# A decoder layer on one core: score tiles, bank split, weight pool and transpose path changed together

## The chip, the core and the metric

The kernel runs on one of the eight cores of a Trainium2 chip. The metric is device time in microseconds (us) for one execution. Times given for a kernel without further words are medians of several runs; views of the profile come from one profiled execution. The names of the engines are those of the profile: PE is TensorE's matmul side (PEld its weight loads), DVE is VectorE, ACT is ScalarE, POOL is GpSimd, SP is SyncE, which here does nothing but issue DMAs.

## The reference

Everything is fp32. Three blocks follow each other, each with its own layer norm and residual, on `x` of shape (4, 1024, 256):

```python
x = x + self_attention(layernorm(x))      # 16 query heads, 4 key/value heads of 64, softmax over 1024 keys, not causal
x = x + cross_attention(layernorm(x), ctx)  # 16 heads of 16, 64 context rows
x = x + routed_ffn(layernorm(x))          # the router picks one of 64 small splines for each row

# self-attention
xq = xq * scale;  xk, xv = repeat(xk, 4), repeat(xv, 4)
scores = einsum('bqhd,bkhd->bhqk', xq, xk)
probs  = softmax(scores)
out    = einsum('bhqk,bkhd->bqhd', probs, xv).reshape(B, S, 1024) @ o_w.T + o_b
```

The 4 x 16 x 1024 x 1024 scores of the self-attention are nearly all of the work.

## The kernel before

**Tiles and steps.** For each of the 4 batch rows there are 8 query tiles of 128 rows. Heads are taken in pairs: the two heads of a pair lie on partitions 0-63 and 64-127 (`halves`) and use a key/value head each. A *step* is one pair of heads with one query tile; two steps make a *duo* (function `duo`, L566): four heads, 4 x 1024 weights per query row. There are 256 steps and 128 duos.

**One step.** Four matmuls (L592) fill two score tiles `s` of 128x1024, one for each head and two PSUM banks each. For each tile DVE finds the negated row maximum (`nmax`, L606) and ACT takes the exponential (L612), which writes the weights into the duo's tile `prob` (128x4096) and adds the row sums into `sums`. The next step's scores need both tiles free, since there are two in all.

**Turning the weights.** The value product AV (L671) contracts over keys, so it needs the weights with the keys on partitions. There are two ways. Where `by_array(d)` holds (every fourth duo, L458), PE turns 128x128 blocks with an identity (`ptp`, L631, a "flip") into PSUM and ACT copies them (L635) into `probT`. In the other duos DVE transposes the 32x32 blocks in place (L621, one instruction for a head), and sixteen DMAs, the carries (L648), move the blocks between groups of 32 partitions from `prob` to `probT`:

```python
643            for k in range(4):
644                for qb in range(4):
645                    r = (qb + k) % 4
...
648                        nc.sync.dma_start(
649                            out=probT.t[32 * r : 32 * r + 32, S * qb : S * (qb + 1)],
650                            in_=prob.t[32 * qb : 32 * qb + 32, S * r : S * (r + 1)],
651                        )
```

Every carry waits for all four transposes of its duo, and AV for all sixteen carries. There are two `prob` and two `probT` tiles.

**After AV.** AV runs in two parts of eight matmuls into a PSUM tile `av` (L659), ACT copies it to `heads` (L686). When the four duos of a query tile are there, `project` (L691) divides by the row sums, which travel through DRAM to be spread over partitions (`rsT`, `rsD`, `rb`), and multiplies by the output weights (`po`, L728).

**Everything else** is spread between these steps: layer norms with their transposes (`ln_pt`, L441), projections of queries (`pq`, L545), keys and values (`pk`, `pv`), cross-attention for two query tiles at a time (`pxq`, `xs`, `pxt`, `xav`, `pxp`, L797), and the feed-forward for four query tiles at a time (`pch`, `pcomp`, `pr` and a long series of small DVE operations, L1023; nine calls).

**PSUM.** Eight banks: `ps_s` has two tiles of two banks for the scores, `ps_1` three single banks (tag `p1`, function `psum1`) for all of the rest but AV, and `ps_o` one for AV. `xs` takes two of the single banks at once.

**The order.** Nothing is scheduled by hand or by the compiler: each operation is handed to a planner with `add(engine, cost, key, emit, reads, writes, ...)`. `Flow.order` (L120) simulates the six queues with the given costs, a lag from one engine to the next (`LAG`, L87), a count of places for each kind of tile (`places`, L228), and always emits the operation that could start first; among equals an `urgent` one, then the lower key. Tiles of one kind are taken in order of the keys of their first users, unless the kind is in `shared`. An operation that isn't urgent is put off if an urgent one would come up while it runs (L153):

```python
153                        if not t.urgent and start < soon < start + t.cost - self.SLACK:
154                            start = soon
```

What the planner emits is the program order of each engine; at run time the semaphores decide, and each queue keeps that order. Places are counted in the plan only: the pools hand out their buffers in turn.

Of the kernel before, what the change touches and what calls it, by code (L numbers as in the profile page):

```python
# [56 lines left out]
class Buf:  # L57


    def __init__(self, tag=None, make=None, whole=None):  # L60
        self.tag, self.make, self.whole = tag, make, whole or self
        self.writers, self.readers, self.parts = [], [], {}
        self.uses, self.first, self.left, self.last, self.t = set(), None, 0, 0.0, None

# [13 lines left out]
class Flow:  # L78
# [7 lines left out]
    AHEAD, SLACK = 16, 0.4  # L86
    LAG = {"PE": 0.3, "DVE": 0.2, "ACT": 0.25, "POOL": 0.25}  # L87
# [32 lines left out]
    def order(self):  # L120
        free = {tag: [0.0] * n for tag, n in self.places.items()}
# [14 lines left out]
        while todo:  # L136
            best = None
            for engine, some in could.items():
                pick = None
                soon = min((t.ready for t in some if t.urgent), default=inf)  # L140
                for t in some:
                    if t.key > front + self.AHEAD:
                        continue
                    start = max(now[engine], t.ready)
                    seen = {}
                    for b in t.takes:
                        k = seen[b.tag] = seen.get(b.tag, -1) + 1
                        line = self.lines.get(b.tag)
                        if len(free[b.tag]) <= k or (line and line[k] is not b):
                            break  # L150
                        start = max(start, free[b.tag][k])
                    else:
                        if not t.urgent and start < soon < start + t.cost - self.SLACK:  # L153
                            start = soon
                        rank = (start, not t.urgent, t.key, t.number)
                        if pick is None or rank < pick[0]:
                            pick = (rank, t)
                if pick and (best is None or pick[0] < best[0]):
                    best = pick
# [5 lines left out]
            for b in t.takes:  # L165
                free[b.tag].pop(0)
# [10 lines left out]
            for b in t.bufs:  # L177
                b.left -= 1
                b.last = max(b.last, t.end)
                if not b.left:  # L180
                    insort(free[b.tag], b.last + 0.2)
            yield t

    def emit(self):
        for t in self.order():
            for b in t.takes:
                b.t = b.make()
# [5 lines left out]
def decoder(  # L193
# [26 lines left out]
    ps_s = ctx.enter_context(tc.tile_pool(name="ps_s", bufs=2, space=PSUM))  # L220
    ps_1 = ctx.enter_context(tc.tile_pool(name="ps_1", bufs=3, space=PSUM))
    ps_o = ctx.enter_context(tc.tile_pool(name="ps_o", bufs=1, space=PSUM))
# [5 lines left out]
            s=2, p1=3, o=1, x=3, xn1=2, xT=1, kT0=1, kT1=1, vn=4, qT=12, prob=2, probT=2, sums=3, nmax=4,  # L228
# [8 lines left out]
    def buf(tag, pool, *shape, bufs=None, name=None):  # L237
        bufs = flow.places[tag] if bufs is None else bufs
        return Buf(tag, lambda: pool.tile([P, *shape], F32, tag=tag, name=name or tag, bufs=bufs))

    def psum1(name):

        return Buf("p1", lambda: ps_1.tile([P, 512], F32, tag="p1", name=name))
# [159 lines left out]
    def layernorm(key, name, src, dst, w, reads, writes):  # L403

        st = Buf("ln", lambda: (
            small.tile([P, w, 6], F32, tag="bnst", name=f"{name}_st", bufs=2),
            small.tile([P, w, 2], F32, tag="bnmv", name=f"{name}_mv", bufs=2),
            small.tile([P, w], F32, tag="bnrs", name=f"{name}_rs", bufs=2),
# [20 lines left out]
        add("DVE", 0.6 * w, key, stats, reads, [st], holds=writes)  # L429
        add("POOL", 1.0, key, rsqrt, [st], [st])  # L430
        add("ACT", 0.45 * w, key, apply, [st, *reads], writes)

    def transposed(key, name, src, dst, k, reads, write):
# [12 lines left out]
        add("PE", 0.55, key, flips, reads, [pt], holds=[write])  # L446
# [9 lines left out]
    def by_array(d):  # L456

        return d % 4 == 3  # L458
# [27 lines left out]
    def keys(b, j, key):  # L486

        kT = kTs[b, j] = buf(f"kT{j}", big, S, name=f"kT_{b}_{j}")
        for g in range(2):
# [15 lines left out]
            add("PE", 1.75, key, project, [wk_, xTs[b].part(2 * g), xTs[b].part(2 * g + 1)], [pk], holds=[kT])  # L505
            add("ACT", 0.7, key, evict, [pk, colv_], [kT])

    def value_rows(b, g, key):
# [24 lines left out]
        add("PE", 1.75, key, project, [wv_, xTs[b].part(g)], [pv], holds=[vn])  # L533
        add("DVE", 0.69, key, evict, [pv, rowv_], [vn])

    def queries(b, w, c, key):
# [16 lines left out]
        add("PE", 1.8, key, project, [wq_, xTs[b].part(w)], [pq], holds=[qTs[b, w, c], qTs[b, w, c + 1]])  # L553
# [12 lines left out]
    def duo(b, d):  # L566
# [7 lines left out]
        prob = Buf("prob", lambda: work.tile([P, 4 * S], F32, tag="prob", name=f"prob_{b}_{d}"))  # L574
        probT = Buf("probT", lambda: work.tile([P, 4 * S], F32, tag="probT", name=f"probT_{b}_{d}"))
# [7 lines left out]
        for i in range(2):  # L583
# [3 lines left out]
            ps = [Buf("s", lambda z=z: ps_s.tile([P, S], F32, tag="s", name=f"s_{b}_{d}_{i}_{z}")) for z in range(2)]  # L587
# [12 lines left out]
            add("PE", 1.95, n - 3, scores, [q, kT], ps, holds=[prob, ss], lead=True)  # L600
            for z in range(2):
# [14 lines left out]
                add("DVE", 1.22, n - 3, largest, [ps[z]], [nmax], urgent=True)  # L616
                add("ACT", 1.33, n - 3, exponential, [ps[z], nmax], [prob.part((z, i)), ss.part(k)], urgent=True)
                if not by_array(d):
# [4 lines left out]
                    add("DVE", 1.25, n - 1, turn, [prob.part((z, i))], [prob.part((z, i))])  # L623
                else:
                    for g in range(2):
# [11 lines left out]
                        add("PE", 0.54, n - 1, flips, [prob.part((z, i))], [pt], holds=[probT])  # L637
                        add("ACT", 0.6, n - 1, evict, [pt], [probT.part((z, g))])

        if not by_array(d):  # L640


            for k in range(4):
                for qb in range(4):
                    r = (qb + k) % 4

                    def carry(qb=qb, r=r):
                        nc.sync.dma_start(  # L648
# [5 lines left out]
                        "SP", 0.6, at, carry, [prob.part((z, i)) for z in range(2) for i in range(2)],  # L654
# [4 lines left out]
        av = Buf("o", lambda: ps_o.tile([P, 2 * P], F32, tag="o", name=f"av_{b}_{d}"))  # L659
        jp = e // 2  # L660
        for part in range(2):
            def values(part=part):
                for kc in range(4 * part, 4 * part + 4):
                    for z, r in enumerate(halves):
# [3 lines left out]
                        else:  # L668
# [3 lines left out]
                            av.t[r, :],  # L672
# [7 lines left out]
                "PE", 1.9, at + 1, values,  # L680
# [4 lines left out]
        def evict():  # L685
            nc.scalar.copy(hd.t.rearrange("p c q -> p (c q)"), av.t)  # L686

        add("ACT", 0.45, at + 1, evict, [av], [hd])


    def project(b, qt):  # L691
# [4 lines left out]
        rT = Buf("rsT", lambda: small.tile([H, P], F32, tag="rsT", name=f"rsT_{b}_{qt}", bufs=1))  # L696
        rD = Buf("rsD", lambda: dram.tile([2, QC, P], F32, tag="rsD", name=f"rsD_{b}_{qt}"))
# [21 lines left out]
        for z, r in enumerate(halves):  # L719
            add("SP", 0.5, at - 4, lambda z=z, r=r: spread(z, r), [rD], [rb.part(z)], lag=2.5)  # L720
        for e in range(QC // 2):
            add("POOL", 0.6, at - 1, lambda e=e: divide(e), [rb.part(0), rb.part(1), hT[e]], [hT[e]])
        xb = x_part(b, qt)
        po, t = psum1(f"po_{b}_{qt}"), buf("res", work, D, name=f"res_{b}_{qt}")
        for part in range(2):
# [4 lines left out]
            add("PE", 1.75, at, out_rows, hT[2 * part : 2 * part + 2] + [wo_] + [po] * part, [po], holds=[t])  # L730
# [66 lines left out]
    def cross_attention(b, t0, at):  # L797
# [27 lines left out]
        add("PE", 1.8, at + 1, project_q, [xT, xwq_], [pq], holds=[qT])  # L825
# [3 lines left out]
        for k in range(TX):  # L829
# [15 lines left out]
            add("PE", 1.1, now, scores, [qT, kblk], ps, holds=[sc])  # L845
            for z in range(2):
# [9 lines left out]
                add("DVE", 0.75, now, masked, [ps[z], mneg_], [sc])  # L856
# [30 lines left out]
            add("POOL", 1.6, now + 1, add_up, [sc], [half], holds=[rs])  # L887
# [34 lines left out]
            add("PE", 0.9, now + 3, values, [pT.part(0), pT.part(1), vblk], [av], holds=[oT])  # L922
# [18 lines left out]
            add("PE", 0.9, now + 4, project_o, [oT, xwo_], [po], holds=[r])  # L941
# [4 lines left out]
    def calibrated(at, name, score, w, reads):  # L946
# [3 lines left out]
        def new(tag, *shape):  # L950
            return small.tile([P, *shape], F32, tag=tag, name=f"{name}_{tag}", bufs=1)

        c = Buf("cal", lambda: (
            new("cf", n), new("chot", NK - 1, n), new("clow", n), new("cpick", NK - 1, n), new("cval0", n), new("cval1", n),
# [45 lines left out]
    def first_max(at, name, g, n, reads):  # L1000

        m = Buf("fm", lambda: (
            small.tile([P, n], F32, tag="fm", name=f"{name}_m", bufs=4),
            small.tile([P, n, NCL], F32, tag="fw", name=f"{name}_w", bufs=4),
# [18 lines left out]
    def feed_forward(b, t0, w, at):  # L1023
# [3 lines left out]
        xf = Buf("xf", lambda: big.tile([P, w, D], F32, tag="xf", name=f"ln3_{name}_n"))  # L1027
        xT = Buf("fxT", lambda: big.tile([P, DC, n], F32, tag="fxT", name=f"ln3_{name}_T"))
# [13 lines left out]
        hT = Buf("hT", lambda: big.tile([COMP, n], F32, tag="hT", name=f"hT_{name}"))  # L1042
        ph, pc = psum1(f"pch_{name}"), psum1(f"pcomp_{name}")
        comp = Buf("comp", lambda: small.tile([P, w, 2], F32, tag="comp", name=f"comp_{name}", bufs=2))
# [26 lines left out]
        sc = Buf("sc", lambda: small.tile([P, w, NS], F32, tag="sc", name=f"sc_{name}", bufs=1))  # L1071
        pr = psum1(f"pr_{name}")

        def route():
# [18 lines left out]
        hot = Buf("hot", lambda: (  # L1093
            small.tile(wide, F32, tag="hot", name=f"hot_{name}", bufs=1),
            small.tile([P, w, TPC], F32, tag="sel", name=f"sel_{name}", bufs=2),
            small.tile([P, w], F32, tag="tno", name=f"tno_{name}", bufs=1),
            small.tile([P, w], mybir.dt.int32, tag="tile", name=f"tile_{name}", bufs=1),
# [22 lines left out]
        par = Buf("par", lambda: big.tile([P, w, GT], F32, tag="par", name=f"par_{name}"))  # L1120
        for t in range(w):
# [8 lines left out]
            add("POOL", 1.2, at + 11, gather, [hot], [par.part(t)], lag=3.0)  # L1130


        hh = Buf("hh", lambda: (
            small.tile([P, w, GRID], F32, tag="hh", name=f"hh_{name}", bufs=1),
            small.tile([P, w, GRID], F32, tag="h2", name=f"h2_{name}", bufs=1),
            small.tile([P, w], F32, tag="mag", name=f"mag_{name}", bufs=1),
# [166 lines left out]
```

## Time and profile before

| | us |
|---|---|
| median of 3 runs | 1982.43 (1979.98 to 1986.18) |
| the profiled execution, own time | 1978.13 |
| its span, first to last instruction | 1976.4 |
| PE busy | 1737.7 |
| DVE busy | 1400.9 |
| ACT busy | 1062.5 |
| POOL busy | 554.1 |
| first scores start at | 36.8 |
| last scores start at | 1867.4 |
| mean granted TensorE clock | 0.939 |

Busy times are unions over an engine's instructions; issuing DMAs isn't in them. The row of a group has the busy time of all its instructions, the mean duration of one in ns, and the engine's idle time just before them with the instruction that ended it. fp32 matmuls appear as two records each, so a step's four score matmuls are eight records.

### The profile page before, as it was taken

How to read it: one execution, taken by the hardware profiler on the slowest of the kernel's cores; microseconds unless marked ns; L12 is line 12 of the kernel's file. 1: busy time of each engine (PE TensorE's matmuls, PEld its weight loads, DVE VectorE, ACT ScalarE, POOL GpSimd, SP SyncE). 2: the span in 40 equal slices, each digit the busy share in tenths (PEclk: the TensorE clock that was granted, in tenths of full speed). 3: DMA queues.
4: the chain of work that ended last, by engine and by line, in shares of the span. 5: the costliest groups of instructions: out<-in, count | busy, mean ns of one | idle time of the engine just before them, and what ended most of it. 6: DMA issues, size and time to landing. Idle time of an engine off the chain costs nothing.

```text
span 1976.4 us, 28894 instructions
## 1 busy us (share of the span) xinstructions
PE 1737.7 (88%) x10180; PEld 1025.7 (52%) x10180; DVE 1400.9 (71%) x2036; ACT 1062.5 (54%) x1977; POOL 554.1 (28%) x872
## 2 busy tenths in 40 slices
PE   6898989889998998989999898988999899997842
PEld 4455555555654555555655454555555455554521
DVE  4667777886778766787677676787677876778632
ACT  3445556656564655655565555655565455555511
POOL 1001213152122512225031522316122350304352
PEclk8889999999998999999999898999999899999965
DMA  3566455455655455566454456545555645445500
GB/s 131 128 139 150 115 140 122 115 146 125 138 129 136 106 137 124 121 152 150 102 134 107 123 136 139 139 116 126 136 116 116 157 118 129 105 111 130 139 23 12
DMA packets 95455, 243.05 MB, mean 123 GB/s; under 512 B 28368, under 2 KB 39376, under 8 KB 95312
## 3 DMA queue, kind: packets, MB, share of 16 engines
q1 hardware_dynamic: 91504, 229.39, 49.6%
q0 software_dynamic: 2704, 9.46, 1.7%
q10 hardware_dynamic: 1104, 2.37, 0.3%
q8 instruction: 81, 1.33, 0.3%
q14 instruction: 62, 0.51, 0.1%
HBM read 35.32 MB, written 4.46 MB: 20 GB/s over the span
## 4 chain that ended last, share of the span: by engine, by line
PE 64%; DVE 16%; ACT 6%; POOL 5%; DMA 3%; SPq 3%; issue 3%; POOLq 0%; DVEq 0%; ACTq 0%
PE s L592 22%; PE av L671 18%; DVE nmax L606 6%; PE pq L545 5%; PE po L728 4%; PE ptp L631 4%; DVE prob L621 3%; SPq L648 3%; ACT prob L612 3%; PE pk L494 1%; PE pv L517 1%; DMA par<-in_table,tile 1%; PE pxt L898 1%; PE xs L837 1%; PE pxq L814 1%
## 5 line engine op out<-in xcount | busy, mean ns | idle before, releaser
L606 DVE TENSOR_REDUCE nmax<-s 128x1 f32<-128x1024 f32 x512 | 601.9, 1216 | 342.7 <-PE s L592 341.4
L612 ACT ACTIVATE prob<-s,nmax 128x1024 f32<-128x1024 f32 x512 | 568.8, 1114 | 407.3 <-DVE nmax L606 388.7
L592 PE MATMUL s<-kT,qT 64*128 64x512 f32 x2048 | 584.4, 639 | 35.0 <-ACT prob L612 34.6
L671 PE MATMUL av<-probT,vn 128*64 128x256 f32 x4096 | 499.4, 396 | 29.5 <-DMA probT<-prob 26.0
L621 DVE STREAM_TRANSPOSE prob<-prob 128x1024 f32<-128x1024 f32 x384 | 458.6, 1223 | 37.7 <-ACT prob L612 26.8
L671 PEld LDWEIGHTS av<-probT,vn 128*64 128x64 f32 x4096 | 298.2, 142 | 252.3 <-issue 111.7
L592 PEld LDWEIGHTS s<-kT,qT 64*128 64x128 f32 x2048 | 212.9, 192 | 266.5 <-issue 163.6
L710 POOL TENSOR_TENSOR heads<-heads,rb 128x256 f32<-128x256 f32 x128 | 90.0, 729 | 607.6 <-DMA rb<-rsD 503.7
L635 ACT COPY probT<-ptp 128x512 f32<-128x512 f32 x256 | 137.8, 590 | 74.3 <-PE ptp L631 72.5
L631 PE MATMUL ptp<-ident,prob 128*128 128x128 f32 x1024 | 141.1, 281 | 34.0 <-ACT prob L612 30.4
L631 PEld LDWEIGHTS ptp<-ident,prob 128*128 128x128 f32 x1024 | 112.8, 143 | 82.4 <-issue 37.6
L545 PE MATMUL pq<-ln_T,wq 128*128 128x256 f32 x512 | 127.6, 394 | 12.3 <-DVE xsc L849 12.3
L863 POOL TENSOR_TENSOR xsc<-xsc,xmx 128x1024 f32<-128x1024 f32 x32 | 61.2, 1914 | 248.2 <-DVE xmx L860 136.7
L728 PE MATMUL po<-wo,heads 128*128 128x256 f32 x512 | 119.2, 383 | 1.6 <-POOL heads L710 1.6
L545 PEld LDWEIGHTS pq<-ln_T,wq 128*128 128x128 f32 x512 | 95.3, 194 | 47.9 <-issue 29.2
L728 PEld LDWEIGHTS po<-wo,heads 128*128 128x128 f32 x512 | 95.5, 190 | 29.8 <-POOL heads L710 9.2
L612 ACT ACTIVATION_READ_ACCUMULATOR prob<-s,nmax 128x1 f32 x512 | 101.0, 197 | 0.0
L427 ACT ACTIVATE ln_n<-x,ln_mv,ln_rs 128x256 f32<-128x256 f32 x64 | 36.6, 596 | 107.1 <-POOL ln_mv L422 107.1
L686 ACT COPY heads<-av 128x256 f32<-128x256 f32 x128 | 47.6, 372 | 76.3 <-PE av L671 73.9
L556 ACT ACTIVATE qT<-pq,bqs,qscale 128x256 f32<-128x256 f32 x128 | 65.6, 564 | 35.6 <-PE pq L545 35.5
L419 POOL TENSOR_SCALAR ln_rs<-ln_mv 128x1 f32<-128x1 f32 (+1 forms) x96 | 21.4, 222 | 213.2 <-DVE ln_mv L415 200.7
L441 PE MATMUL ln_pt<-ident,ln_n 128*128 128x128 f32 x192 | 37.2, 312 | 44.9 <-ACT ln_n L427 42.4
(166 smaller groups left out, 1498.1 us busy)
## 6 DMA issues: line engine op xcount, KB each, us to landing
probT<-prob SPq DMA_DIRECT2D x1536, 128.0 KB, 2.3
rb<-rsD SPq DMA_DIRECT2D x64, 256.0 KB, 3.9
ln_n<-in_x SPq DMA_DIRECT2D x16, 256.0 KB, 3.1
x<-in_x SPq DMA_DIRECT2D x8, 512.0 KB, 4.9
out<-ln_n POOLq DMA_DIRECT2D x7, 512.0 KB, 4.9
wq<-in_w_qT ACTq DMA_DIRECT2D x1, 1024.0 KB, 8.0
wo<-in_w_oT SPq DMA_DIRECT2D x1, 1024.0 KB, 12.6
rowv<-in_rows ACTq DMA_DIRECT2D x1, 774.0 KB, 10.6
```

What stands on the lines that cost most here:

```text
L545: mm(pq.t[:, 2 * P * k : 2 * P * (k + 1)], lhsT=wq[:, dc, (c + k) * P : (c + k + 1) * P], rhs=xTs[b].t[:, dc, 2 * P * w : 2 * P * (w + 1)] ...
L556: nc.scalar.activation(qTs[b, w, c + k].t, pq.t[:, 2 * P * k : 2 * P * (k + 1)], AF.Identity, bias=bqs[:, c + k : c + k + 1], scale=qscale,)
L592: mm(ps[z].t[:, 512 * g : 512 * (g + 1)], lhsT=q.t[r, (qt % 2) * P : (qt % 2 + 1) * P], rhs=kT.t[r, 512 * g : 512 * (g + 1)], start=True, ...
L606: nc.vector.tensor_reduce(nmax.t, ps[z].t, AX.X, ALU.max, negate=True)
L612: nc.scalar.activation(weights(prob.t, z, i), src, AF.Exp, bias=nmax.t, accum_out=ss.t[:, k : k + 1])
L621: nc.vector.transpose(t, t)
L631: flip(pt.t[:, j * P : (j + 1) * P], weights(prob.t, z, i)[:, kc * P : (kc + 1) * P], ident)
L635: nc.scalar.copy(to[:, z, 4 * g : 4 * g + 4, i, :], pt.t.rearrange("p (c q) -> p c q", q=P))
L671: mm(av.t[r, :], lhsT=vns[b, kc // 2].t[:, kc % 2, j * HD : (j + 1) * HD], rhs=rhs, start=(kc == 0), stop=(kc == NT - 1),)
L710: nc.gpsimd.tensor_tensor(hT[e].t, hT[e].t, rb.t[:, 2 * e : 2 * e + 2, :], ALU.mult)
L728: mm(po.t[:, :D], lhsT=hT[c // 2].t[:, c % 2], rhs=wo[:, c, :], start=(c == 0), stop=(c == QC - 1))
L863: nc.gpsimd.tensor_tensor(sc.t, sc.t, mx.t.unsqueeze(2).to_broadcast([P, XH, SK]), ALU.subtract)
```

## The change

- **Score tiles.** `ps_s` has three tiles of two banks, still one for each head. `ps_1` has two single banks instead of three, and AV takes one of them (`psum1`) instead of its own.
- **Weight tiles.** `prob` and `probT` come from one pool of four tiles.
- **Transposes.** `by_array` is always false: every duo is turned by DVE and carried by DMA; PE's flips and their copies are gone.
- **Two queues.** Of a duo's sixteen carries the last four (`k == 3`) are issued on ACT's queue, the other twelve on SP's as before.
- **Buffers by place.** The planner notes which place a tile was given, and the tile is made from that place's own buffer (`f"{tag}_{k}"`, one buffer each), so plan and program use the same one.
- **Planner.** The rule at L153 is dropped; lags between engines are about halved; a place is free 0.1 us after its last use instead of 0.2; some twenty costs are changed by a few hundredths to half a us.

The core of the diff; the new tags of all other tiles follow the same pattern:

```diff
-    AHEAD, SLACK = 16, 0.4
-    LAG = {"PE": 0.3, "DVE": 0.2, "ACT": 0.25, "POOL": 0.25}
+    AHEAD = 16
+    LAG = {"PE": 0.15, "DVE": 0.1, "ACT": 0.1, "POOL": 0.15}
...
-        free = {tag: [0.0] * n for tag, n in self.places.items()}
+        free = {tag: [(0.0, k) for k in range(n)] for tag, n in self.places.items()}
...
-                soon = min((t.ready for t in some if t.urgent), default=inf)
...
-                        if not t.urgent and start < soon < start + t.cost - self.SLACK:
-                            start = soon
...
-                free[b.tag].pop(0)
+                b.place = free[b.tag].pop(0)[1]
...
-                    insort(free[b.tag], b.last + 0.2)
+                    insort(free[b.tag], (b.last + 0.1, b.place))
...
-                b.t = b.make()
+                b.t = b.make(b.place)
...
-    ps_s = ctx.enter_context(tc.tile_pool(name="ps_s", bufs=2, space=PSUM))
+    ps_s = ctx.enter_context(tc.tile_pool(name="ps_s", bufs=1, space=PSUM))
     ps_1 = ctx.enter_context(tc.tile_pool(name="ps_1", bufs=3, space=PSUM))
-    ps_o = ctx.enter_context(tc.tile_pool(name="ps_o", bufs=1, space=PSUM))
...
-            s=2, p1=3, o=1, x=3, xn1=2, xT=1, kT0=1, kT1=1, vn=4, qT=12, prob=2, probT=2, sums=3, nmax=4,
+            s=3, p1=2, x=3, xn1=2, xT=1, kT0=1, kT1=1, vn=4, qT=12, prob=4, sums=3, nmax=4,
...
     def by_array(d):
 
-        return d % 4 == 3
+        return False
...
-        prob = Buf("prob", lambda: work.tile([P, 4 * S], F32, tag="prob", name=f"prob_{b}_{d}"))
-        probT = Buf("probT", lambda: work.tile([P, 4 * S], F32, tag="probT", name=f"probT_{b}_{d}"))
+        prob = Buf("prob", lambda k: work.tile([P, 4 * S], F32, tag=f"prob_{k}", name=f"prob_{b}_{d}", bufs=1))
+        probT = Buf("prob", lambda k: work.tile([P, 4 * S], F32, tag=f"prob_{k}", name=f"probT_{b}_{d}", bufs=1))
...
-            add("PE", 1.95, n - 3, scores, [q, kT], ps, holds=[prob, ss], lead=True)
+            add("PE", 1.93, n - 3, scores, [q, kT], ps, holds=[prob, ss], lead=True)
...
-                add("DVE", 1.22, n - 3, largest, [ps[z]], [nmax], urgent=True)
-                add("ACT", 1.33, n - 3, exponential, [ps[z], nmax], [prob.part((z, i)), ss.part(k)], urgent=True)
+                add("DVE", 1.17, n - 3, largest, [ps[z]], [nmax], urgent=True)
+                add("ACT", 1.14, n - 3, exponential, [ps[z], nmax], [prob.part((z, i)), ss.part(k)], urgent=True)
...
-                    add("DVE", 1.25, n - 1, turn, [prob.part((z, i))], [prob.part((z, i))])
+                    add("DVE", 1.19, n - 1, turn, [prob.part((z, i))], [prob.part((z, i))])
...
-                    def carry(qb=qb, r=r):
-                        nc.sync.dma_start(
+                    engine, queue, cost = ("ACT", nc.scalar, 0.45) if k == 3 else ("SP", nc.sync, 0.68)
+
+                    def carry(qb=qb, r=r, queue=queue):
+                        queue.dma_start(
...
-                        "SP", 0.6, at, carry, [prob.part((z, i)) for z in range(2) for i in range(2)],
+                        engine, cost, at, carry, [prob.part((z, i)) for z in range(2) for i in range(2)],
...
-        av = Buf("o", lambda: ps_o.tile([P, 2 * P], F32, tag="o", name=f"av_{b}_{d}"))
+        av = psum1(f"av_{b}_{d}")
```

## The prediction

> **What bounds the kernel now.** I read the page's busy line first, then the busy time in three stretches, then the groups of instructions with the waits in front of them, then SP's own waits and the DMA in one burst. The page:
>
> ```profile
> PE 1737.7 (88%) x10180; PEld 1025.7 (52%) x10180; DVE 1400.9 (71%) x2036; ACT 1062.5 (54%) x1977; POOL 554.1 (28%) x872
> PE 64%; DVE 16%; ACT 6%; POOL 5%; DMA 3%; SPq 3%; issue 3%; POOLq 0%; DVEq 0%; ACTq 0%
> ```
>
> TensorE is the busiest engine and holds 64% of the chain that ended last; VectorE comes next. The busy times by stretch (engines in the order PE, PEld, DVE, ACT, POOL, then clock, DMA share, GB/s) cut the span at the first scores (37 us) and the last scores (1867 us):
>
> ```profile
> 37.00:1867.00 1830.00, 1675.28 (x9901) 985.42 (x9903) 1351.64 (x1844) 1026.39 (x1910) 506.98 (x767) 0.96 0.55 128
> 0.00:37.00 37.00, 21.26 (x58) 12.46 (x60) 10.92 (x54) 13.13 (x25) 7.88 (x44) 0.86 0.52 175
> 1867.00:1976.00 109.00, 41.13 (x227) 27.80 (x223) 38.36 (x138) 22.99 (x43) 39.28 (x61) 0.63 0.06 17
> ```
>
> The middle decides: PE 1675 of 1830 us (91.5%), 155 us idle; DVE 1352 us (74%). Its 256 steps (one per pair of heads and query tile) take 7.15 us each. The head and the tail are latency and hardly change. The groups (busy, mean ns | idle just before, and who ended it):
>
> ```profile
> L606 DVE TENSOR_REDUCE nmax<-s 128x1 f32<-128x1024 f32 x512 | 601.9, 1216 | 342.7 <-PE s L592 341.4
> L592 PE MATMUL s<-kT,qT 64*128 64x512 f32 x2048 | 584.4, 639 | 35.0 <-ACT prob L612 34.6
> L671 PE MATMUL av<-probT,vn 128*64 128x256 f32 x4096 | 499.4, 396 | 29.5 <-DMA probT<-prob 26.0
> L621 DVE STREAM_TRANSPOSE prob<-prob 128x1024 f32<-128x1024 f32 x384 | 458.6, 1223 | 37.7 <-ACT prob L612 26.8
> L635 ACT COPY probT<-ptp 128x512 f32<-128x512 f32 x256 | 137.8, 590 | 74.3 <-PE ptp L631 72.5
> L631 PE MATMUL ptp<-ident,prob 128*128 128x128 f32 x1024 | 141.1, 281 | 34.0 <-ACT prob L612 30.4
> ```
>
> DVE's 342.7 us of waiting are for scores, so PE paces it. PE's own waits are small and each has an owner: 35.0 us of scores waiting for an exponential to free a score tile, 34.0 in front of the flips of every fourth duo, 29.5 in front of AV. Last, the carries:
>
> ```profile
> SPq L648 <- DVE prob L621: 386.2, 84, 11.1
> probT<-prob SPq DMA_DIRECT2D x1536, 128.0 KB, 2.3
> 1073.00:1082.00 9.00, 5.95 (x26) 3.92 (x24) 8.61 (x18) 3.39 (x6) 0.72 (x1) 1.00 0.88 198
> ```
>
> SP waits 386 us for transposes, so it has room. Inside one burst of 16 carries (10.06 us in the timeline) the 16 DMA engines are already 0.88 busy at 198 GB/s.
>
> **What the Trainium skill says.** "DMA: Bandwidth & Descriptors", section "Issuing engines are not separate DMA queues": DMAs of SP and ACT run on the same 16 engines, and a second issuer saves only issue time. The 0.88 of that burst agrees: the second queue can shorten it by about an eighth at most, 10.1 to 9 us. "TensorE: Matmul & The Clock Gate", "What's actually happening": the clock halves after about 3.4 us of idle time. Agrees: after 3.25 us idle at 618.71 us, eight score matmuls took 4.91 us, against 1.99 without a gap. The same page, "Architectural detail", calls ACT and DVE strict FIFO, so a carry on ACT holds up what stands behind it; no run here shows a carry on ACT. "PSUM — Partial Sum Buffer", "PSUM: the matmul accumulator", counts 8 banks: 4+3+1 become 6+2, with none left over; the trace cannot show banks.
>
> **The change, part by part.**
> *Flips out.* 32 duos lose 1024 flips: −141.1 us of PE, all on the bounding engine, and −34.0 us of waits in front of them. On ACT their 256 evictions (137.8 us) go too.
> *Block transposes in.* 32 × 4 = 128 more, × 1.223 = +156.5 us of DVE. Middle: PE 1675−137 (the flips that lie in it) = 1538, DVE 1352+156 = 1508. They are now equal, and DVE's slack of 26% falls to 10%. It is no direct cost, since it lies in the 342.7 us that DVE waited. The cover is thin, though: a maximum (L606) more often meets a transpose and waits half of 1.22 us. Extra chance (0.90−0.74) × 0.61 × 512 = 50 us; I let half reach PE: +25 (bounds 0 and 100).
> *Carries.* 16 × 32 = 512 more DMAs. SP keeps its number (12 × 128 = 1536, median issue 0.59 us, so 7.1 us a duo of 12.9). ACT gets 4 × 128 = 512, at the 0.45 us of its weight loads at the start: +230 us of queue. ACT: 1062−138+230 = 1154 us, under the other two, so nothing while DVE is on time; behind an ACT carry that waits for a late transpose stand exponentials, and PE waits for those. That is in the +25. DMA share 0.55 × 4/3 over a shorter time is about 0.8: a longer landing than 2.3 us, which goes into AV's 29.5 us of waits. I leave these unchanged: later landings against one pool of four tiles. That pool lets the next duo take a tile before the last carry has been read; no row shows this wait apart (bounds −26 and +30).
> *Third score tile.* One head of the next step can start after the first exponential. Of 35.0 us of waits I take 70%: −25 (bounds −35 and 0).
> *Two banks for all the rest.* Takes after: AV 128, pq 64, xs 64, pxt 64, ln_pt 48, po, pxp, xav, rsT 32 each, others 83: 579, which share two banks instead of three plus AV's own. PE fills them 1738−141−584 = 1013 us. Adding an eviction and about half a us of waiting to each fill gives some 1760 us of occupancy, so 1.3 us of turnover a take, and two banks are 53% full over 1670 us (before: about 29% of three). Before, only pq and pxp waited for a bank behind xs (12.8 us). I take +25, 0.04 us a take; bounds 0 and 240 (rival C).
> *Clock.* The mean score matmul was 639 ns against a median of 589; fewer long gaps: −10 (bounds −40, +20).
> *Last duo.* It was a flipped one. Now: two last transposes 2.4, twelve issues 7.1, landing 2.3 put its AV about 6 us later: +6.
> *Order.* The planner's costs, shorter lags and the dropped reservation for urgent work move queues around; no row prices this: 0, within ±30.
>
> Sum against the profiled span: 1976.4−141.1−34.0−25−10+25+25+6 = 1822. Its own time was 1978.1, 1.7 above the span; the median of the runs shown is 1982.4, 4.3 above that. So **1828 us**. The middle becomes about 1670 us: PE 92%, DVE 90%, 6.5 us a step.
>
> **The rivals.**
> A, *the cushions work*: three score tiles and four weight tiles cover DVE and banks, and PE reaches 94%: 1538/0.94 = 1636, +37 +115 = 1788, 1794 as a median. For: PE's idle time before is mostly short waits with owners that go. Against: DVE at 92%.
> B, *DVE becomes the bound in bursts*: the router and spline work of the feed-forward (9 calls) kept DVE full between 600 and 628 us already; there PE stood 3.25 us. If each call holds the scores 8 us longer than planned: +72, 1900.
> C, *two banks starve PE* (slower): the 272 short fills (ln_pt, xs, pxt, xav, pxp, rsT, some 0.65 us each) don't cover a turnover of 1.3, and each loses 0.65 us: 177; AV, which now must find a bank of 128, loses 0.5: 64. 241 in place of 25: 2044. It decides against the change once the mean loss passes (25+154)/579 = 0.31 us a take. For: xs takes both banks at once. Against: PE has scores, a third of its time, to put between, and few bank waits with three.
> D, *the second queue does nothing*, as the engines are 0.88 busy anyway: then AV is ready a us later, hidden by the pool; 1830.
>
> **How the numbers follow.** The likeliest with D 0.50, A 0.24, B 0.13, C 0.13. A measurement here tells 0.3% (6 us) from no change. Faster: all but C and a sliver, 0.85; same 0.03; slower 0.12. Range 1750 to 1925: below A and above B by the bounds of the unknown costs; left out is C and a little at the low end.
>
> **What would show it.** Right: no L631 and L635 groups; 512 transposes of 1.22 us, about 615 us; PE near 1590 and DVE near 1555 busy; waits of DVE for scores down from 341 to some 150; waits of scores for exponentials under 15; 2048 carries, 512 of them on ACT. Wrong: AV, pq or pxt waiting over 150 us in total for heads copies, pq evictions or the masked scores (C); PE waiting over 150 us behind L606 and L621 (B); AV waiting over 100 us for carries (the pool or the DMA).

## The result and the profile after

| | before | after |
|---|---|---|
| median of 20 runs each, us | 1979.41 (1968.99 to 1986.18) | 1969.97 (1954.94 to 1979.67) |
| ratio, 95% interval | | 0.9951 [0.9933, 0.9969] |
| span of the profiled execution, us | 1976.4 | 1968.0 |
| from the first to the last scores, us | 1830.6 | 1787.4 |
| from there to the end, us | 109 | 143 |

The change gains half a per cent; 7.8% was forecast. The page after, busy line and chain:

```profile
PE 1664.0 (85%) x9156; PEld 936.4 (48%) x9156; DVE 1535.9 (78%) x2164; ACT 929.0 (47%) x1721; POOL 556.0 (28%) x872
PE 40%; DMA 19%; DVE 14%; SPq 12%; ACT 5%; issue 5%; POOL 3%; ACTq 2%; DVEq 0%; POOLq 0%
```

The flips are gone (10180 − 1024 = 9156 records), but TensorE's share of the chain falls from 64% to 40%, and DMA and SP's queue, 3% each before, have 31%. No engine became the bound; the experiments below show that the carries did. The middle and the tail (columns as in the prediction):

```profile
37.00:1825.00 1788.00, 1588.27 (x8833) 889.54 (x8831) 1478.52 (x1958) 888.69 (x1650) 496.18 (x750) 0.94 0.69 166
1825.00:1968.00 143.00, 55.32 (x271) 34.39 (x269) 46.42 (x153) 27.29 (x47) 52.12 (x79) 0.61 0.18 46
```

The DMA share of the middle rose from 0.55 to 0.69. PE stands 200 us of it, 155 before. The groups:

```profile
L601 DVE TENSOR_REDUCE nmax<-s 128x1 f32<-128x1024 f32 x512 | 599.4, 1211 | 192.8 <-PE s L587 191.2
L616 DVE STREAM_TRANSPOSE prob<-prob 128x1024 f32<-128x1024 f32 x512 | 612.1, 1221 | 69.7 <-ACT prob L607 56.6
L668 PE MATMUL av<-probT,vn 128*64 128x256 f32 x4096 | 543.6, 420 | 110.3 <-DMA probT<-prob 50.8
L587 PE MATMUL s<-kT,qT 64*128 64x512 f32 x2048 | 583.8, 628 | 34.7 <-ACT prob L607 34.7
```

The wait in front of AV (L668) rose from 29.5 to 110.3 us, and AV itself takes 44 us more than before. The waits of SP's queue:

```profile
SPq L645 <- DMA probT<-prob: 340.8, 289, 5.3
SPq L645 <- DVE prob L616: 113.1, 25, 31.9
...
SPq L645 <- PE av L668: 80.1, 15, 14.9
```

Before, SP waited 386 us for transposes: the data came last. Now it waits 341 us for earlier carries and 80 us for AV to give a tile back. The landings of both queues are longer than the 2.3 us of before:

```profile
probT<-prob SPq DMA_DIRECT2D x1536, 128.0 KB, 3.1
probT<-prob ACTq DMA_DIRECT2D x512, 128.0 KB, 3.7
```

A duo's life, worked out from the two traces (means in us, good to about a tenth): *from the last transpose to the last landing* 12.4 before, 16.1 after; *from there to AV* 2.8 and 3.7; a duo's two weight tiles are held for 43.8 us in all before and 50.7 after. Four tiles give 4 × 14.03 = 56.1 us per duo at the pace of the kernel after, so they are held nine tenths of the time. The 14.03 us are the mean distance of two duos' first scores.

### The profile page after: what moved, and what is told of

The parts are those of the page before. It is cut to its first block, busy times and chain, and to the rows that moved or that the text cites. A ratio compares the mean times of both kernels' runs of the same rounds, so it can differ in the third digit from the quotient of the medians.

```text
span 1968.0 us, 27927 instructions
## 1 busy us (share of the span) xinstructions
PE 1664.0 (85%) x9156; PEld 936.4 (48%) x9156; DVE 1535.9 (78%) x2164; ACT 929.0 (47%) x1721; POOL 556.0 (28%) x872
## 4 chain that ended last, share of the span: by engine, by line
PE 40%; DMA 19%; DVE 14%; SPq 12%; ACT 5%; issue 5%; POOL 3%; ACTq 2%; DVEq 0%; POOLq 0%
PE av L668 16%; DMA probT<-prob 16%; PE s L587 12%; SPq L645 11%; DVE nmax L601 6%; PE po L725 3%; ACT prob L607 3%; DVE prob L616 3%; ACTq L645 2%; DMA rb<-rsD 1%; PE pq L540 1%; PE pk L489 1%; PE pxt L895 1%; PE pxp L929 1%; PE pv L512 1%
## 5 line engine op out<-in xcount | busy, mean ns | idle before, releaser
L601 DVE TENSOR_REDUCE nmax<-s 128x1 f32<-128x1024 f32 x512 | 599.4, 1211 | 192.8 <-PE s L587 191.2
L616 DVE STREAM_TRANSPOSE prob<-prob 128x1024 f32<-128x1024 f32 x512 | 612.1, 1221 | 69.7 <-ACT prob L607 56.6
L668 PE MATMUL av<-probT,vn 128*64 128x256 f32 x4096 | 543.6, 420 | 110.3 <-DMA probT<-prob 50.8
L587 PE MATMUL s<-kT,qT 64*128 64x512 f32 x2048 | 583.8, 628 | 34.7 <-ACT prob L607 34.7
L668 PEld LDWEIGHTS av<-probT,vn 128*64 128x64 f32 x4096 | 321.1, 151 | 349.6 <-issue 183.4
L725 PE MATMUL po<-wo,heads 128*128 128x256 f32 x512 | 125.5, 389 | 1.7 <-POOL heads L707 1.4
L540 PEld LDWEIGHTS pq<-ln_T,wq 128*128 128x128 f32 x512 | 94.2, 192 | 35.8 <-issue 11.1
L882 POOL TENSOR_TENSOR xsc<-xsc,xrs 128x1024 f32<-128x1024 f32 x32 | 60.8, 1901 | 56.5 <-DVE xrs L879 56.0
L895 PE MATMUL pxt<-ident,xsc 128*128 128x128 f32 x256 | 43.9, 302 | 36.0 <-POOL xsc L882 31.1
L1120 POOL DMA_INDIRECT par<-in_table,tile x32 | 32.4, 1012 | 128.8 <-DVE tile L1109 122.9
```

The costliest lines, as they stand in the source:

```text
L540: mm(pq.t[:, 2 * P * k : 2 * P * (k + 1)], lhsT=wq[:, dc, (c + k) * P : (c + k + 1) * P], rhs=xTs[b].t[:, dc, 2 * P * w : 2 * P * (w + 1)] ...
L587: mm(ps[z].t[:, 512 * g : 512 * (g + 1)], lhsT=q.t[r, (qt % 2) * P : (qt % 2 + 1) * P], rhs=kT.t[r, 512 * g : 512 * (g + 1)], start=True, ...
L601: nc.vector.tensor_reduce(nmax.t, ps[z].t, AX.X, ALU.max, negate=True)
L616: nc.vector.transpose(t, t)
L668: mm(av.t[r, : 2 * P], lhsT=vns[b, kc // 2].t[:, kc % 2, j * HD : (j + 1) * HD], rhs=rhs, start=(kc == 0), stop=(kc == NT - 1),)
L725: mm(po.t[:, :D], lhsT=hT[c // 2].t[:, c % 2], rhs=wo[:, c, :], start=(c == 0), stop=(c == QC - 1))
```

## The experiments

Every ratio is to the kernel before, measured beside it. The experiments ran on several chips in five groups, so differences of 0.3% between groups aren't read. A run that changes places or tasks is also ordered anew by the planner; e1, e10, e11, e16 and e17 keep the order of the kernel after, and e13 that of the kernel before.

**e1, one queue.** ACT's four carries go to SP; the order of the other work is kept.

```diff
-  engine, queue, cost = ("ACT", nc.scalar, 0.45) if k == 3 else ...
+  engine, queue, cost = ("ACT", nc.sync, 0.45) if k == 3 else ...
```

> The changed kernel with its order as planned, but the four carries of a duo that ACT issued are issued by SP, at the place that the plan gave them. Queue theory (the two queues share completion counters, so that SP's carries wait for ACT's): SP's waits for carries fall from 341 us to under 80, from last transpose to last landing 12 to 13 us instead of 15.5, ACT no longer waits for carries (50 us), time 1860 to 1920. DVE theory (VectorE, at 78% with unfilled gaps, paces all) and bank theory: 1955 to 1985, as SP only gets more to issue.

Measured 1.0213 [1.0175, 1.0251], 2018.87 us. The theory that the second queue was the harm fell: it is worth 2.6%. In the list of waits:

```profile
PE av L668 <- DMA probT<-prob: 97.8, 31, 5.5
```

It was 50.8 in the kernel after. SP's waits for carries fell from 340.8 to 176.4, not under 80 as that theory had it.

**e2, flips back** (`by_array` gives `d % 4 == 3` again, all else as after).

> The changed kernel with every fourth duo turned by TensorE again (by_array as before). DVE theory: VectorE is relieved of 153 us and the time falls below the changed kernel's, 1900 to 1940. Queue theory: a quarter fewer carries, so SP's waits for carries fall by a quarter or more, but PE gets 141 us back: 1945 to 1990. Bank theory: 256 more takes of the two single banks, slower, 2000 or more.

Measured 1.0042 [1.0023, 1.006]: PE busy 1744.4, DVE 1391.2. AV waits only 15.7 us for carries, and still the time is 0.9% above the kernel after. TensorE has 80 us more to do than after, which fits a kernel that it paces again.

**e3, banks back** (`s=2, p1=3, o=1`, AV in its own bank).

> The changed kernel with the bank split of before: two score tiles, three single banks, one bank for AV. Bank theory (two banks starve PE): faster, 1880 to 1930, PE's idle time before pq, pxp, ln_pt, pxt and AV down by half. Queue and DVE theories: no gain; with only two score tiles the waits of scores for exponentials rise from 35 us: 1965 to 2010.

Measured 1.0071 [1.0045, 1.0097]. The page's group of scores:

```profile
L587 PE MATMUL s<-kT,qT 64*128 64x512 f32 x2048 | 659.9, 672 | 88.6 <-ACT prob L607 88.1
```

The third score tile takes this wait from 88.1 to 34.7 us. The run gives back tile and banks together, so it can't price the banks alone; for those the waits of the kernel after speak: AV waits 0.9 us for a copy of `heads`, `pxp` 11.1 for masked scores, `pq` 1.5 in all. Two banks for the rest don't hold the kernel back.

**e4, two pools** (`prob=2, probT=2`).

> The changed kernel with two prob and two probT tiles instead of one pool of four. Pool theory (in the pool a carry or an exponential is planned into a tile whose last carries have not been read yet): the waits of the first carry of a duo for earlier carries go, and the time falls to 1900 to 1945. Queue and DVE theories: slower by 1 to 3% (1985 to 2030), since a prob tile is then reused after two duos instead of three places.

Measured 1.0058 [1.0035, 1.0082]. Exponentials wait 103.0 us for carries to leave `prob` (49.9 after). The common pool is worth about 1.1%. This wait alone isn't the price: e10, below, has 102.6 us of it and the time of the kernel after.

**e5 and e6, a fifth tile and its control.** Both make room: `qT=8`, `x=2`, and halves of `wq` and `wo` are used twice. e5 has `prob=5`, e6 `prob=4`.

> The changed kernel with a fifth tile in the weight pool. To make room, qT has 8 places and x 2, and the kernel keeps only half of wq and of wo and uses each half twice (so the projections multiply by other columns, with the same instructions). Pool theory (a weight tile lives 29.7 us as prob, from first exponential to last landing, and 21.0 as probT; 50.7 us on four tiles allow no period under 12.7 us a duo, against 14.0 measured, so that every late carry is felt): time falls to 1880 to 1930. Carry theory (the sixteen carries of a duo take 12.4 us from first issue to last landing, and the DMA engines set that): carries no faster and the time 1940 to 1970. DVE theory: 1955 to 1985.

> The control for the five tiles: four tiles with the same smaller qT and x and the same halves of wq and wo. All theories: as the changed kernel, 1955 to 1985; a difference shows what a re-planned order alone is worth.

Measured e5 0.9715 [0.9684, 0.9746], e6 0.9891 [0.9843, 0.9938]. The fifth tile is worth 1.8% (e5 against e6; the order planned anew, e6 against the kernel after, 0.6%): the lives of the tiles are part of the bound, but not most of what is missing.

**e7, planner alone.** The kernel before with the new lags, costs and buffers by place; flips, pools, banks and queue as before.

> The kernel before with the planner's part of the change alone: new costs, shorter lags, no reservation for urgent work, buffers by place; flips in every fourth duo, two pools, the old banks and one queue stay. Order theory (the new planner settings lose what the other parts gain): slower than before by 1 to 3%, 2000 to 2040. Pool and carry theories: within 0.7% of before, 1965 to 1993.

Measured 0.9866 [0.984, 0.9892], 1955.01 us: faster than the whole change. TensorE has 61% of the chain. The parts that the change is about lose 0.9% together (0.9951 / 0.9866).

**e8, landing planned.** A place is planned as free when the carry that reads it has landed, not when it has been issued. The edit holds for every DMA with a lag above 1 us:

```diff
-  b.last = max(b.last, t.end)
+  b.last = max(b.last, t.end + (t.lag if t.lag > 1 else 0.0))
```

> The changed kernel, in which the planner frees a tile when the last carry out of it has landed (2.3 us after the end of its issue) and not when it was issued. Pool theory in its planner's form (carries and exponentials are planned into tiles that are still being read): the 3.7 us from the last transpose to the first carry fall under 2, SP's waits for carries fall from 341 us to under 250, time 1930 to 1955. Carry and DVE theories: 1960 to 1985.

Measured 0.9792 [0.977, 0.9815], 1940.76 us: the fastest complete kernel here, 1.6% below the one after. The chain of waits:

```profile
PE 51%; DVE 17%; DMA 11%; ACT 6%; SPq 6%; issue 4%; POOL 4%; ACTq 1%; DVEq 0%; POOLq 0%
```

DMA and SP's queue fall from 31% to 17%. SP's waits are not those that the pool theory had named:

```profile
SPq L645 <- DMA probT<-prob: 489.0, 359, 5.9
SPq L645 <- PE av L668: 14.5, 5, 5.5
```

The waits for earlier carries rise from 340.8 to 489.0 us instead of falling, so they are no measure of the loss; the waits for AV to give a tile back fall from 80.1 to 14.5. The order of work is worth 1.6%. That it gains by counting on fewer tiles that aren't free yet fits the second wait and isn't shown apart.

**e9, exchange alone.** e7 with `by_array` false: all duos by blocks on one queue, two pools, old banks.

> The kernel before with the new planner settings (as in e7), and every duo turned by block transposes; two pools of two, the old banks and one queue stay. Against e7 (0.987 of before) it shows what the exchange of the transposes does by itself. Pool theory (a prob tile lives some 25 us; with two of them and no short-lived flipped duo between, a duo takes 13 us at least and every late carry is felt): slower than e7 by 2 to 4%, 1995 to 2040. PE theory of the prediction (PE is the bound and loses 141 us): faster than e7, 1850 to 1900.

Measured 1.008 [1.0041, 1.012], 2.2% above e7. Taking 1024 flips from the bounding engine lost time. DMA share 0.70; exponentials wait 119.0 us for carries. With the other parts of the change in place the same exchange gains 0.9% (the kernel after against e2): what it is worth hangs on pool, queue and banks.

**e10, half of each transpose.** `t = t[:, :, :4]` ahead of `nc.vector.transpose(t, t)`, else as after.

> The changed kernel, order as planned, in which each block transpose turns only half of the columns of its head (the other half is carried untransposed): DVE loses some 300 us of busy time. DVE theory: 1840 to 1890. Pool theory: only the 4.7 us from the last exponential to the last transpose shorten, to about 3, so a tile lives 51 minus 2 us: 1920 to 1950. Carry theory: 1945 to 1970.

Measured 0.9946 [0.9926, 0.9965]. The busy line:

```profile
PE 1660.1 (84%) x9156; PEld 938.7 (48%) x9156; DVE 1284.4 (65%) x2164; ACT 928.5 (47%) x1721; POOL 555.1 (28%) x872
```

VectorE has 251 us less to do and the time is that of the kernel after: VectorE is not what bounds the kernel after.

**e11, half carries.** Each carry moves half of its bytes, the first head's of each pair, and AV reads that half for both heads:

```diff
-  out=probT.t[32*r : 32*r+32, S*qb : S*(qb+1)]
+  out=probT.t[32*r : 32*r+32, S*qb : S*qb + S//2]     # in_ likewise
```

> The changed kernel, order as planned, in which each carry moves only half of its columns (64 KB for 128; the product reads the carried half twice, with the same matmuls). Carry theory (the bytes and the DMA engines set the pace): from the first issue to the last landing 12.4 us fall to 9, time 1860 to 1910. Pool theory: both lives shorten by some 3 us: 1890 to 1925. DVE theory: 1950 to 1975.

Measured 0.9406 [0.938, 0.9432], 1861.34 us. The same instructions in the same order take 5.5% less. Busy line, chain and the stretch from the first to the last scores:

```profile
PE 1634.2 (88%) x9156; PEld 916.4 (49%) x9156; DVE 1531.5 (82%) x2164; ACT 929.9 (50%) x1721; POOL 555.6 (30%) x872
```
```profile
PE 54%; DVE 17%; DMA 9%; SPq 6%; ACT 5%; issue 4%; POOL 4%; ACTq 1%; DVEq 0%; POOLq 0%
```
```profile
37.00:1724.00 1687.00, 1557.76 (x8829) 869.48 (x8829) 1473.18 (x1955) 888.89 (x1649) 495.07 (x749) 0.96 0.39 98
```

The middle takes 1687 us with PE at 92% (1557.76 / 1687): nearly the middle that the prediction had described (1670 us, 92%). AV and SP's waits:

```profile
L668 PE MATMUL av<-probT,vn 128*64 128x256 f32 x4096 | 517.4, 405 | 43.2 <-issue 21.4
SPq L645 <- DMA probT<-prob: 178.0, 167, 6.9
SPq L645 <- DVE prob L616: 114.1, 42, 12.9
```

AV waits 67 us less than in the kernel after and takes 26 less. The edit does one more thing: with only the first head's half to carry, a carry waits for two of a duo's four transposes. In the trace 46 of 128 duos begin to carry before their last transpose has ended (none in the kernel after), mostly by 1.1 us. How much of the gain is this earlier start and how much the bytes wasn't tried apart. For the bytes speak that SP's waits for transposes are as long as after (113.1) while those for carries halve, that shorter transposes alone gain nothing (e10), and that in e15 117 of 128 duos start early and the gain is 1.1%.

**e12, eight carries on each queue**, on top of e8 (`k >= 2` in place of `k == 3`).

> The changed kernel with the landing in the plan (as in e8, 0.979 of before), and eight of the sixteen carries on ACT's queue instead of four. Carry theory with issue as its limit: carries shorter, 1900 to 1930. If the two queues hold each other up at the shared counters: no shorter, ACT's exponentials behind waiting carries, 1945 to 1990.

Measured 1.0037 [1.0007, 1.0067], 2.5% above e8. SP's waits, and ACT's:

```profile
SPq L645 <- DMA probT<-prob: 635.0, 347, 9.1
```
```profile
ACT prob L607 <- DMA probT<-prob: 161.8, 39, 7.5
```

In e8 SP waited 489.0 us. In the program the carries of both queues signal the same eight counters in turn, and a carry waits for the DMA before it on its counter. The queues so hold each other up, and on ACT exponentials stand behind the wait. Other runs agree: with one queue and two pools (e9) SP's carries don't wait for earlier ones at all, with two queues and two pools (e4) 206.6 us. The common pool brings such waits too: 176.4 us on one queue (e1).

**e13, e14, e15: half carries in the kernels that lose or lack something.** The edit of e11, made in the kernel before, in e7 and in e9.

> The kernel before with each carry cut to half its bytes (64 KB; AV reads the half that was carried for both heads, in the three of four duos that are carried). Theory (the carries' DMA time became a bound only when all duos were carried): this kernel has TensorE as its bound and 25% fewer carries, so it gains little, 0.98 to 1.0 of the kernel before. Rival (light carries help any such kernel alike): 0.93 to 0.95, as in e11.

> The planner's settings alone (e7, 0.987 of the kernel before) with half carries: the pair to e15. Theory: 0.965 to 0.985, about 1% below e7, TensorE busy over 90% of the span. Rival (light carries help alike): 0.93.

> The exchange of transposes alone on top of the planner's settings (e9, 1.008 of the kernel before) with half carries. Theory: with light carries the exchange gains what TensorE is rid of: 0.93 to 0.95, 2 to 4% below e14, where with whole carries it lost 2.2% (e9 against e7). Rival (two score tiles, one queue and the pools hold the exchange back, not the bytes): 0.98 or more, no better than e14.

Measured e13 0.9932 [0.9913, 0.9951], e14 0.9884 [0.9844, 0.9924], e15 0.9973 [0.9956, 0.999]. e13 answers as the theory had it: with flips in every fourth duo light carries gain 0.7%. e14 gains nothing over e7 (0.9866), where the theory had 1%. e15 contradicts it: light carries give the exchange alone only 1.1%, and it still lies 0.9% above e14, so the bytes can't be its whole price. Its group of scores and SP's first wait:

```profile
L587 PE MATMUL s<-kT,qT 64*128 64x512 f32 x2048 | 635.3, 669 | 56.2 <-ACT prob L607 52.8
```
```profile
SPq L645 <- DVE prob L616: 308.1, 97, 29.6
```

SP waits for transposes, not for carries, as it did in e9; the exponentials' waits for carries fall from 119.0 to 25.6 us. The scores wait for exponentials, and from the first issue to the end of the sixteenth one queue still takes 11.3 us of a duo of 14.3 (from the trace; 11.2 in e9 with whole carries).

**e16, half carries and half transposes**, both in the kernel after.

> The kernel after with half carries and with each transpose on half of its columns as well (VectorE some 250 us lighter; half of the weights are left unturned). What bounds it once the carries are light? If VectorE, the prediction's second bound: 0.91 or less of the kernel before, 3% or more below e11 (0.941). If TensorE: 0.935 to 0.945, as e11.

Measured 0.9221 [0.9186, 0.9256], 2.0% below e11 (0.9221 / 0.9406): between the two expectations. With light carries VectorE's load does cost something, some 37 us (0.0185 of 1979).

**e17 and e18, e11 without the second queue, and without the third score tile.** The edits of e1 and of e3 in e11.

> e11 (half carries, 0.941 of the kernel before) with all sixteen carries on SP's queue, the same order of each engine's other work. If the issue of sixteen carries on one queue is the next limit: 0.98 or more, most of e11's gain gone, AV waiting for carries over 40 us. If the third score tile is what e15 lacked: 0.94 to 0.96.

> e11 (half carries, 0.941 of the kernel before) with two score tiles, three single banks and AV's own, as in the kernel before. If the third score tile is what e15 lacked: 0.97 or more, scores waiting for exponentials over 50 us. If the queue is: 0.94 to 0.955.

Measured e17 0.9892 [0.9875, 0.991], e18 0.9736 [0.9711, 0.9761]. Light carries gain most beside both parts; taking the queue away costs more than taking the tile with its bank split. The chain of e17, then e18's scores:

```profile
PE 45%; SPq 24%; DVE 12%; DMA 7%; issue 5%; ACT 4%; POOL 3%; POOLq 0%; DVEq 0%; ACTq 0%
```
```profile
L587 PE MATMUL s<-kT,qT 64*128 64x512 f32 x2048 | 664.3, 668 | 90.6 <-ACT prob L607 87.0
```

On one queue SP's issue holds 24% of the chain; with two score tiles the handshake of PE, DVE and ACT comes back. All pairs in one table:

| kernel | whole carries | half carries |
|---|---|---|
| before | 1.000 | 0.993 (e13) |
| planner alone | 0.987 (e7) | 0.988 (e14) |
| planner and exchange | 1.008 (e9) | 0.997 (e15) |
| after, one queue | 1.021 (e1) | 0.989 (e17) |
| after, old banks | 1.007 (e3) | 0.974 (e18) |
| after | 0.995 | 0.941 (e11) |

In the left column the planner, the queue and the score tile with its banks are worth 1 to 3% each; in the right one the queue is worth 4.9% and the tile with its banks 3.4%. The carries' weight covers what the other parts could give, and those parts cover what lighter carries could give.

## Why the prediction was wrong

**The step that failed: carries, costed at nothing.** The prediction had all the figures: 16 × 131072 B = 2.10 MB a duo, 198 GB/s in a burst, so 10.6 us of DMA for a duo that it put at 2 × 6.5 = 13 us. It saw a share of about 0.8 and "a longer landing than 2.3 us", and bounded the effect at −26 and +30, as a wait in front of AV. The runs show 109 us for half of their weight (1970.0 − 1861.3, e11, the earlier start included), against 14 us (0.7%) in the kernel before. What it missed is that the carries are a stage of the pipeline, not a latency: a duo's carries took 12.4 us from first issue to last landing (10.4 + 2.0) of a period of 14.0, and two tiles are held meanwhile. A stage so full has little room left when anything else is late, and delays a later duo; this reading fits e5, e8 and e11. Its pool bound priced only the old wait, not the new one.

**TensorE's busy time, −141.1.** It fell by 73.7 (1737.7 to 1664.0), 67 short; 44 of these are AV's, whose mean rose from 396 to 420 ns, with the minimum and the median at 379 in both traces. AV starts after waits more often now (matmul records above 500 ns went from 217 to 600), and then runs at half the clock: the Trainium skill, "TensorE: Matmul & The Clock Gate", "What's actually happening", says that the clock halves after idling, and these two lines of the timeline agree, the first after a gap of 6.17 us, the second without one (start, duration; the granted clock in the two stretches is 0.50 and 1.00):

```profile
1843.05 3.68 PE L668 MATMUL av<-probT,vn 128*64 128x256 f32 x16 [6.17 <-DMA rsD<-rsT]
1847.42 1.95 PE L668 MATMUL av<-probT,vn 128*64 128x256 f32 x16
```

The step "Clock", −10, had the wrong sign for the same cause: the mean granted clock went from 0.939 to 0.916. The mean score matmul did get shorter (639 to 628 ns), but AV's got longer by more. The idle stretch that the prediction set beside that page's 3.4 us was itself 3.25 us.

**The waits in front of the flips, −34.0,** went, and 80.8 us of new waiting in front of AV (110.3 − 29.5) took their place.

**Block transposes.** 615 us forecast, 612.1 measured; DVE 1535.9 against 1555. That they cost nothing directly is right (e10). The coupling of +25 is of the size of what e16 shows once carries are light, 37 us for half of every transpose (251 us of VectorE, where the step priced 156 more); with whole carries it is hidden.

**Third score tile, −25.** The scores' waits didn't fall (35.0 to 34.7), yet with two tiles and the old banks they are 88.1 (e3). That fits a tile and a coupling that cancel, as in the sum; no run shows either alone. DVE's wait for scores fell to 191.2, near the 150 forecast.

**Two banks, +25,** was too much, and rival C fell: `pq` and `po` stand 1.5 and 1.7 us, AV 0.9 for a copy of `heads`, and going back to three and one (with two score tiles) makes the kernel slower (e3). Rival B fell with e10.

**Second queue.** The prediction gave it a tenth of the burst and rival D nothing. It is worth 2.6% with whole carries (e1) and 4.9% with half ones (e17 against e11). It isn't a matter of the bytes, which are the same: the 0.88 of the burst was read as the limit of the transfer, but the issue of sixteen carries on one queue was a second limit right behind it. ACT's issues took 0.61 us (median), not the 0.45 assumed. More of it isn't better (e12).

**Last duo, +6.** The stretch after the last scores grew by 34 us. The last AV came 12.9 us after the last scores before (flips need no carry) and 43.1 us after. The step counted one duo's issue and landing; the AVs of three duos and the carries of two still stood in line.

**Order, 0 within ±30.** The planner's settings alone gave 1.3% (e7), 26 us, inside the bounds; on top of them the rest of the change loses 0.9%. The change without them was not run. Telling the planner of the landing gave another 1.6% (e8).

In sum: span 1822 forecast, 1968.0 measured, 146 too low, of it 28 in the tail (143 − 115) and 118 in the middle (1788 − 1670). Half carries alone bring the middle to 1687. None of the thresholds under "wrong" was reached by name: AV's waits for carries read 50.8 of 110.3, and another part of the loss lies in AV's slower matmuls. The theory that bytes alone are the cause fell with e15; what stands is that lighter carries gain most, and that one queue's issue and the waits of scores for exponentials are close behind. e11's span of 1862.0 is 40 us above the 1822 forecast, 17 of them in the middle and 23 in the tail (138 − 115); what causes these was not tried apart.

## What to carry to other kernels

When work moves off the busiest engine, price the queue and the DMA that take it up as a stage with a period of its own, bytes over the measured rate and issues times their duration, and compare both with the period that you forecast. Here a stage of 12.4 us in a period of 14.0 was not hidden, with no engine above 85% busy. Ask how many buffers that stage holds and for how long, and whether the order of work counts them as free at the issue or at the landing. Where several parts are within some per cent of the same period, test a part with the next limit already taken away: alone, each looked worth little here.

## What was not expected of the hardware

The time to issue a DMA didn't depend on the bytes here: the median issue of a carry on SP took 0.59 us with 128 KB (e9) and with 64 KB (e15), and the sixteen of a duo, waits between them included, 11.2 and 11.3 us. Two queues whose DMAs signal one set of counters waited for each other: with eight carries on each, SP waited 635.0 us for earlier carries (e12), against 489.0 with twelve and four (e8, planned in the same way).
